# Small weights of an output pipeline moved to the right end of SBUF

## The chip, the cores and the metric

The kernel runs on one core of a Trainium2 chip. The metric is device time of one execution in microseconds (us); lower is better. A core has five engines with their own instruction streams: PE (TensorE, matmuls into PSUM), DVE (VectorE), ACT (ScalarE), POOL (GpSimd) and SP (SyncE, which here only issues DMA transfers). ACT issues a few transfers too. Each stream runs in program order; streams wait for each other and for transfers through semaphores.

## The reference

Eight images of 64x64 positions and 96 channels go through two layers. Each layer is a residual block: group norm, a projection to 192 + 192 channels (x and z), a 3x3 depthwise convolution with SiLU on x, a selective scan over the 4096 positions in four directions with 16 states a channel, layer norm, a gate by SiLU of z, and a projection back to 96 channels. Cut to what matters:

```python
xz = x @ in_proj_w.T;  xp, z = xz[..., :Di], xz[..., Di:]
xc = silu(depthwise_conv3x3(xp) + conv_b)
# selective scan, for each of 4 directions:
h = exp(delta * A) * h + delta * B * u
y = sum(h * C) + u * D
# output
y = layernorm(y, norm_g, norm_b)
x = x + (y * silu(z)) @ out_proj_w.T
```

The second layer has the same parts, and its scan comes from a cumulative-sum form whose result is far from zero only near the ends of each direction, so the kernel computes short heads of it.

## The kernel before

**Stages.** For every image `b` the kernel runs `scan_rows` (from L423): the first layer's scan of image `b`, with the short second-layer scan of image `b-1` and the next convolutions woven in. Then `between(b)` (from L1775) runs the output pipeline `out_phase` (from L1461) as a transition to the next scan. There are eight scans and seven transitions (`b` = 0 to 6); a last `finish` ends the program. In the transitions from `b` = 1 on, `out_phase` carries two streams of eight chunks of 512 positions each: the first layer's output of image `b` (chunks 0 to 7), and the second layer's output of image `b-1` (chunks 8 to 15). In the transition after image 0 it carries one. The order of all work is written out by hand: a counter `k` steps through the list `order`, in which each stage of a chunk has a lag (`row` 8, `silu` 7, `product` 9, `project` 10, `end` 10, `store` 11), so stages of several chunks alternate.

**The end of a transition.** The last chunk passes, among others: the second sum of squares on POOL (L1599), the row-picking matmul `ps_r` on PE with weights `w_pick` (L1534), which spreads one row of reciprocal deviations over 96 partitions, the gate SiLU on ACT (L1589, z weights `zw`, bias `zb`, result `sz`), the scaling on DVE (L1610), the affine step on ACT (L1577), the gated product on POOL (L1602, which reads `sz`), the output matmul on PE (L1562), the residual sum on DVE (L1647) and the store, issued from ACT for the second layer (L1648) and from SP for the first (L1703).

**The start of a scan.** SP issues, in this order: dt_rep and dtu_rep (L518), three pairs b_rep and c_rep (L528), the next dt_rep and dtu_rep, the fourth pair, then the low rows x_dbl (L549) and the `edged` rows of a convolution (L1012). The first twelve are 512 KB each. On ACT the scan starts with the copy `drive` (L878) and decays (L861); behind the first two decays stands the step L614 on the result of the matmul `ps_dt` (L602), which reads x_dbl. On DVE each set is one product (L895) and one scan (L908).

**Memory.** Tiles come from pools; pools are stacked from the left end of SBUF or, with `side="right"`, from the right end, and are released when their block ends. A later pool may lie on the bytes of an earlier one; then its first use waits for the last users of the earlier tiles there. `out_phase` puts its short-lived tiles in a pool called `before` (right end, through the argument `brief`) and its other tiles in `final` (left side). Addresses in one partition, in the transitions with two streams:

| tile or pool | bytes |
|---|---|
| `final`: w_pick, zw1, zb, r, sz (three buffers) | 158,368 to 177,120 |
| `before`: zw0, sums, squares, dt0, z0 and others | 182,496 to 229,344 |
| next scan: dt_rep, two buffers | 176,096 to 184,288 |
| next scan: dtu_rep, two buffers | 184,288 to 192,480 |
| next scan: b_rep and c_rep, nine buffers | 192,480 to 229,344 |

The end of sz's third buffer and the beginning of dt_rep's first share 1,024 bytes. In this program the first dt_rep load waits for the last product (L1602) and the last `ps_r` (L1534).

**Transfers.** All transfers of SP and ACT take their completion semaphore from one rotation of eight, in the order in which the program was laid out, and each first waits for the previous transfer on its semaphore.

Of the kernel before, what the change touches and what calls it, by code (L numbers as in the profile page):

```python
# [8 lines left out]
F32 = mybir.dt.float32  # L9
# [6 lines left out]
NB, HH, WW, C = 8, 64, 64, 96  # L16
L = HH * WW
NH = 2
# [35 lines left out]
def two_ss2d_layers(ctx: ExitStack, tc: tile.TileContext, t: dict, out: bass.AP):  # L54
# [92 lines left out]
    def load_late(pool, *names):  # L147
        for name in names:
            w[name] = pool.tile(list(t[name].shape), F32, name=f"w_{name}")
            nc.sync.dma_start(w[name], t[name])  # L150
# [11 lines left out]
    def chunk_stats(st, i, chunk):  # L162
        nc.vector.bn_stats(st[:, i, :], chunk)

    def stats_tile():
        return small.tile([C, L // MM, nc.vector.BN_STATS_DIM], F32, name="bn_st")

    def group_norm_stages(st, bank):

        got = {}  # L170

        def one(name, **more):
            got[name] = small.tile([C, 1], F32, name=f"gn_{name}", **more)
            return got[name]

        def across(name, src):
            got[name] = bank(f"ps_{name}")
            nc.tensor.matmul(got[name][:C, 0:1], w["group"], src, start=True, stop=True)

        def aggregate():  # L180
            got["mv"] = small.tile([C, nc.vector.BN_AGGR_DIM], F32, name="bn_mv")
            nc.vector.bn_aggr(got["mv"], st)

        def means():
            across("pm", got["mv"][:, 0:1])

        def tiny(out, src, func=AF.Identity, **more):
            nc.scalar.activation(out, src, func, **more)
            return out

        def deviations():
            mv, gm = got["mv"], one("less", bufs=2)
            tiny(gm, got["pm"][:C, 0:1], scale=-1.0 / 3.0)
            dev = tiny(one("dev"), mv[:, 0:1], AF.Square, bias=gm)
            tiny(dev, dev, bias=mv[:, 1:2])

        def variances():
            across("pv", got["dev"])

        def variance():  # L200
            tiny(one("gv"), got["pv"][:C, 0:1], scale=1.0 / 3.0, bias=eps_ln[:C])

        def root():

            r, p, gm = one("r", bufs=8), one("p"), one("gm", bufs=8)
            tiny(r, got["gv"], AF.Ln)
            tiny(r, r, AF.Exp, scale=-0.5)
            tiny(p, r, AF.Square)
            tiny(p, p, scale=got["gv"])
            tiny(p, p, scale=-0.5, bias=one_half)  # L210
            tiny(r, r, scale=p)
            tiny(one("shift", bufs=8), got["less"], scale=r)
            tiny(gm, got["less"], scale=-1.0)

        return [aggregate, means, deviations, variances, variance, root], got
# [1242 lines left out]
                    stop=i == NS - 1,  # L1458
                )

    def out_phase(*streams, plan=None, brief=None):  # L1461

# [6 lines left out]
        with (  # L1471
# [7 lines left out]
            chunks = L // MM  # L1479
            n = len(streams) * chunks  # L1480
            brief = brief or pool
            load_late(pool, "pick")
            zw, zb = [], []
            for l, *_ in streams:
                home = brief if l == 0 and len(streams) > 1 else pool
                zw.append(home.tile([C, D], F32, name=f"zw{l}"))
                nc.sync.dma_start(zw[-1], t[f"in{l}"][:, D:])
                zb.append(pool.tile([C, NH], F32, name=f"zb{l}"))
            plan = plan(pmm) if plan else {}
            held = [{} for _ in range(n)]  # L1490
            groups = [{} for _ in range(n // Q)]
# [181 lines left out]
    def first_deltas(b, xc, pool, bank):  # L1673

        units, jobs, sets, x_dbl = parts = scan_parts(b)
        stages = projection(xc, x_dbl, units[0], pool, bank)
        for job in jobs[:NH]:
            stages += ready(xc, x_dbl, job, pool, bank, by_pe=False)
        stages += projection(xc, x_dbl, units[1], pool, bank)
        return parts, [stage for _, stage in stages]  # L1680
# [16 lines left out]
    def finish_first(b, y, st, xpool):  # L1697


        def done(i, ps, x):  # L1700
            nc.vector.tensor_tensor(x, ps, x, ALU.add)
            chunk_stats(st, i, x)
            return lambda: nc.sync.dma_start(x1[b][:, i * MM : (i + 1) * MM], x)  # L1703

        return 0, norm0[b], y, loaded(t["x"][b], xpool), done
# [57 lines left out]
    def second_of(b, pool, brief, xpool, put):  # L1763

        return finish_second(norm1[b], short_sum(b, pool, brief, put), loaded(x1[b], xpool), out[b])

    def planner():
        plan = {}

        def put(step, stage, *args):  # L1770
            plan.setdefault(step, []).append(lambda: stage(*args))

        return plan, put

    def between(b, y):  # L1775

        st = stats_tile()
        xc = maps[b + 1]
        with (
            tc.tile_pool(name="before", bufs=1, side="right") as before,  # L1780
            tc.tile_pool(name="xs", bufs=1) as xpool,
            tc.tile_pool(name="behind", bufs=1) as pool,
        ):
            plan, put = planner()

            streams = [finish_first(b, y, st, xpool)]
            if b >= 1:
                streams.append(second_of(b - 1, pool, before, xpool, put))
            found = {}

            def beside(pmm):
                bank = lambda name: pmm.tile([P, MM], F32, tag="mm", name=name)
                found["parts"], stages = first_deltas(b + 1, xc, before, pmm)
                steps = (1, 2, 2, 3) + (4, 5, 5, 6, 6, 7, 7, 6, 8, 9, 9)
                steps += (8, 9, 9, 10, 10, 11, 12, 14, 15, 16, 16) + (11, 12, 12, 13)
                for step, stage in zip(steps, stages, strict=True):
                    put(step, stage)
                stages, found[1] = group_norm_stages(st, bank)
                put(24, nc.scalar.preload_act_table_set, "natural_log_exp_and_others")
                for step, stage in zip((17, 18, 19, 20, 21, 24), stages, strict=True):  # L1800
                    put(step, stage)
                if b + 2 < NB:
                    ahead = stats_tile()
                    pieces = []

                    def piece(i):
                        pieces.append(before.tile([C, MM], F32, name="x_st", bufs=3))
                        nc.sync.dma_start(pieces[i], t["x"][b + 2][:, i * MM : (i + 1) * MM])

                    for i in range(L // MM):  # L1810
                        put(i + 3, piece, i)
                        put(i + 5, lambda i: chunk_stats(ahead, i, pieces[i]), i)
                    stages, found[0] = group_norm_stages(ahead, bank)
                    for step, stage in zip((13, 14, 15, 16, 17, 18), stages, strict=True):
                        put(step, stage)
                return plan

            out_phase(*streams, plan=beside, brief=before)
            for kind, norm, image in ((1, norm1, b), (0, norm0, b + 2)):
                if kind in found:  # L1820
                    norm[image] = tuple(found[kind][x] for x in ("gm", "r", "shift"))
        return xc, found["parts"]

    def finish(b, y):

        st = stats_tile()
        with tc.tile_pool(name="behind", bufs=1) as pool:
            plan, put = planner()
            streams = [finish_first(b, y, st, pool)]
            if b >= 1:  # L1830
                streams.append(second_of(b - 1, pool, pool, pool, put))
            out_phase(*streams, plan=lambda pmm: plan)
        with tc.tile_pool(name="x1T", bufs=1) as pool1:
            x1T = pool1.tile([C, L], F32, name="x1T")
            nc.sync.dma_start(x1T, x1[b])
            xc = keep.tile([C, NH, L], F32, name="map")
            norm = conv_second(x1T, st, xc)
            with rotating():
                scan_head(xc, worst)
            out_phase(finish_second(norm, xc, kept(x1T), out[b]))  # L1840
# [37 lines left out]
    with tc.manual_schedule():  # L1878
        for b in range(NB):
            y = keep.tile([C, NH, L], F32, name="map")  # L1880
            with (
                tc.tile_pool(name="rows", bufs=1) as rows,
                tc.tile_pool(name="beside", bufs=1) as pool,
            ):
                scan_rows(xc, y, parts, beside(b, pool), rows, pool)
            if b + 1 < NB:
                xc, parts = between(b, y)
# [101 lines left out]
```

## Time and profile before

| what | value |
|---|---|
| runs | 12389.48, 12404.24, 12425.54 us; median 12404.24 |
| the profiled execution | 12404.1 us, its span 12402.2 us |
| busy PE, DVE, ACT, POOL | 77%, 88%, 78%, 85% of the span |
| DMA, share of 16 engines | 44.6% on SP's queue, 0.3% on ACT's |
| granted TensorE clock | 0.803 |
| one POOL product L1602 (96x1024) | 2.35 us |
| one DVE scan L908 (128x1024), with state | 2345 ns |

The span is the time from the first to the last instruction of one profiled execution. A line of the profile's lists names a source line, an engine, the operation with its output and input tiles, a count, the busy time and the mean of one, and then the idle time of that engine just before these instructions, with what ended it (the releaser). The engines are busy most of the time on average, and this average hides the transitions, in which they take turns; a change inside one is read in the order of time.

### The profile page before, as it was taken

What the parts mean: (1) busy time and instruction counts of PE and PEld (TensorE: products, weight loads), DVE (VectorE), ACT (ScalarE), POOL (GpSimd) and SP (SyncE); (2) the same over time, 40 slices, a digit from 0 to 9 for tenths busy, and PEclk for the clock granted to TensorE, in tenths of its full rate; (3) what the DMA queues carried; (4) which work ended last, traced back from release to release, by engine and by line L of the source; (5) the groups of instructions that cost most, each with busy time, mean ns of one, the idle gap of its engine ahead of it and who ended that gap; (6) DMA issues with size and microseconds to landing.
All of it is one profiled execution on the core that took longest, in us unless ns stands there. A gap on an engine that the chain in (4) does not pass through costs nothing. (4 is left out here: it accounts for less than half of the span.)

```text
span 12402.2 us, 134216 instructions
## 1 busy us (share of the span) xinstructions
PE 9540.3 (77%) x44312; PEld 3022.4 (24%) x44312; DVE 10960.4 (88%) x6870; ACT 9688.3 (78%) x15131; POOL 10508.3 (85%) x4802
## 2 busy tenths in 40 slices
PE   5875578787888778877788777888788887886565
PEld 1221122222222222222222222222222222222122
DVE  6999889996999969999799987999879998899976
ACT  4888778887887868878788787887778877788874
POOL 3999889996999969998699986999879987799974
PEclk8887778888888878888888878887788877887786
DMA  3444344444444444444444454444544445444430
GB/s 96 165 155 156 127 159 161 154 156 152 148 164 160 161 138 164 163 162 147 148 156 158 162 165 135 160 162 161 163 138 153 156 156 158 136 165 160 157 123 23
DMA packets 666561, 1853.80 MB, mean 149 GB/s; under 512 B 184936, under 2 KB 199150, under 8 KB 665757
## 3 DMA queue, kind: packets, MB, share of 16 engines
q1 hardware_dynamic: 658685, 1832.52, 44.6%
q10 hardware_dynamic: 7168, 12.59, 0.3%
q8 instruction: 352, 5.77, 0.2%
q14 instruction: 356, 2.92, 0.1%
HBM read 1533.82 MB, written 311.02 MB: 149 GB/s over the span
## 5 line engine op out<-in xcount | busy, mean ns | idle before, releaser
L924 POOL TENSOR_TENSOR out<-set,c_rep 128x1024 f32<-128x1024 f32 x3114 | 7290.0, 2359 | 884.4 <-PE acc L960 317.8
L908 DVE TENSOR_TENSOR_SCAN set<-decay,state,set 128x1024 f32<-128x1024 f32 x2304 | 5366.3, 2345 | 407.4 <-ACT decay L861 189.6
L861 ACT ACTIVATE decay<-dt_rep,w_a 128x1024 f32<-128x1024 f32 x3072 | 3420.2, 1114 | 335.7 <-DVE set L908 329.8
L895 DVE TENSOR_TENSOR set<-drive,b_rep 128x1024 f32<-128x1024 f32 x2346 | 2811.1, 1198 | 43.1 <-DMA b_rep<-x_dblr 28.2
L1027 PE MATMUL ps_conv<-edged,taps 96*96 96x512 f32 (+1 forms) x4032 | 2476.3, 754 | 54.5 <-DVE dt L787 25.9
L960 PE MATMUL acc<-out,w_gather 128*32 128x256 f32 x24576 | 2274.2, 480 | 8.1 <-POOL out L924 7.7
L908 DVE TENSOR_TENSOR_SCAN set<-decay,set 128x1024 f32<-128x1024 f32 x768 | 1744.4, 2286 | 224.5 <-ACT decay L861 146.6
L885 POOL TENSOR_TENSOR set<-dtu_rep,b_rep 128x1024 f32<-128x1024 f32 x768 | 1810.1, 2357 | 93.9 <-DMA b_rep<-x_dblr 51.6
L951 PE MATMUL acc<-map,w_eye 96*32 96x256 f32 x4608 | 568.5, 575 | 1483.4 <-ACT map L990 1253.5
L990 ACT COPY map<-acc 32x256 f32<-32x256 f32 x3072 | 1470.5, 479 | 45.8 <-PE acc L960 5.6
L960 PEld LDWEIGHTS acc<-out,w_gather 128*32 128x32 f32 x24576 | 781.8, 130 | 1939.5 <-issue 1282.0
L1027 PEld LDWEIGHTS ps_conv<-edged,taps 96*96 96x96 f32 (+1 forms) x4032 | 727.5, 200 | 1405.4 <-issue 1244.3
L919 ACT COPY state<-set 128x1 f32<-128x1 f32 x2304 | 426.1, 185 | 754.3 <-DVE set L908 747.9
L634 PE MATMUL ps_sp<-z,w_eye 96*96 96x512 f32 x960 | 658.2, 774 | 288.8 <-ACT ln L643 244.4
L655 POOL TENSOR_TENSOR dtu<-ln,map 96x1024 f32<-96x1024 f32 x256 | 670.7, 2620 | 237.2 <-DVE ln L651 133.0
L878 ACT COPY drive<-dtu_rep 128x1024 f32<-128x1024 f32 (+1 forms) x810 | 808.0, 997 | 34.7 <-DMA dtu_rep<-dtu_far 30.1
L602 PE MATMUL ps_dt<-x_dbl,w_dtw 7*96 7x512 f32 x1024 | 595.4, 663 | 301.2 <-ACT z L615 151.0
L951 PEld LDWEIGHTS acc<-map,w_eye 96*32 96x32 f32 x4608 | 101.4, 121 | 1954.6 <-ACT map L990 1656.1
L634 PE MATMUL ps_sp<-dtu,w_eye 96*96 96x512 f32 x960 | 554.6, 662 | 0.0
L634 PE MATMUL ps_sp<-ln,w_eye 96*96 96x512 f32 x960 | 535.5, 642 | 0.0
L614 ACT ACTIVATE dt<-ps_dt 96x512 f32<-96x512 f32 x512 | 303.0, 592 | 279.2 <-PE ps_dt L602 260.0
L634 PE MATMUL ps_sp<-dt,w_eye 96*96 96x512 f32 x960 | 506.7, 610 | 0.0
(239 smaller groups left out, 9496.8 us busy)
## 6 DMA issues: line engine op xcount, KB each, us to landing
dt_rep<-dt_far SPq DMA_DIRECT2D x768, 512.0 KB
dtu_rep<-dtu_far SPq DMA_DIRECT2D x768, 512.0 KB
b_rep<-x_dblr SPq DMA_DIRECT2D x256, 512.0 KB
c_rep<-x_dblr SPq DMA_DIRECT2D x256, 512.0 KB
b_rep<-x_dblc SPq DMA_DIRECT2D x256, 512.0 KB
c_rep<-x_dblc SPq DMA_DIRECT2D x256, 512.0 KB
dt_far<-ln SPq DMA_DIRECT2D x256, 384.0 KB
dtu_far<-dtu SPq DMA_DIRECT2D x256, 384.0 KB
```

The lines of the kernel that those rows point to most:

```text
L634: nc.tensor.matmul(job["ps"][:C, :], w["eye"], job[term][:, halves[s]], start=i == 0, stop=i == 3,)
L655: nc.gpsimd.tensor_tensor(like(job["dtu"], col), like(job["dt"], col), positions(xc[:, h, :], col, t0, T), ALU.mult,)
L861: nc.scalar.activation(s["decay"], s["group"]["dt"], AF.Exp, scale=rate)
L878: nc.scalar.copy(s["group"]["drive"], s["group"]["dtu"])
L885: nc.gpsimd.tensor_tensor(s["buf"], s["group"]["dtu"], b, ALU.mult)
L895: nc.vector.tensor_tensor(s["buf"], s["group"]["drive"], b, ALU.mult)
L908: nc.vector.tensor_tensor_scan(ordered(s["buf"], unit), ordered(s["decay"], unit), ordered(s["buf"], unit), 0.0 if unit["nth"] == 0 else s ...
L924: nc.gpsimd.tensor_tensor(s["out"], s["buf"], s["unit"]["c", s["i"]], ALU.mult)
L951: nc.tensor.matmul(acc, lhs[:, GC * g : GC * (g + 1)], positions(old[:, h, :], unit["column"], unit["t0"] + at, n), start=True, stop=False ...
L960: nc.tensor.matmul(acc, w["gather"], s["out"][:, at : at + n], start=False, stop=s["i"] == NS - 1, skip_group_check=True,)
L990: nc.scalar.copy(yk, like(acc, unit["column"]))
L1027: nc.tensor.matmul(job["ps"][:C, :], taps[l][:k, h, tap, :], edged[:k, tap // 3 : tap // 3 + rows, tap % 3 : tap % 3 + WW], start=tap == 0 ...
```

## The change

`out_phase` takes one more pool, `late`, and puts w_pick, the z weights zw (except the zw of the first stream, which stay in `brief` when there are two streams) and the biases zb there. `between` opens it on the right side before all other pools of the transition. Without the argument, in `finish` and elsewhere, `late` is `final`, as it was.

```diff
-    def out_phase(*streams, plan=None, brief=None):
+    def out_phase(*streams, plan=None, brief=None, late=None):
...
             brief = brief or pool
-            load_late(pool, "pick")
+            late = late or pool
+            load_late(late, "pick")
             zw, zb = [], []
             for l, *_ in streams:
-                home = brief if l == 0 and len(streams) > 1 else pool
+                home = brief if l == 0 and len(streams) > 1 else late
                 zw.append(home.tile([C, D], F32, name=f"zw{l}"))
                 nc.sync.dma_start(zw[-1], t[f"in{l}"][:, D:])
-                zb.append(pool.tile([C, NH], F32, name=f"zb{l}"))
+                zb.append(late.tile([C, NH], F32, name=f"zb{l}"))
...
         with (
+            tc.tile_pool(name="late", bufs=1, side="right") as late,
             tc.tile_pool(name="before", bufs=1, side="right") as before,
...
-            out_phase(*streams, plan=beside, brief=before)
+            out_phase(*streams, plan=beside, brief=before, late=late)
```

With two streams, `late` then takes 226,976 to 229,344, `before` 180,128 to 226,976, and `final` ends at 174,752. The loops, the operations and their order stay as they are.

## The prediction

> **What bounds the kernel now.** I read the list of what SyncE's queue waited for first, because the diff moves only tiles, and a tile that changes its place can change only waits. Columns: engine and line, what it waited for, us in total, times, longest.
>
> ```profile
> SPq L518 <- PE ps_r L1534: 126.0, 6, 21.6
> SPq L518 <- POOL y L1602: 31.2, 6, 5.2
> ```
>
> L518 is the load of dt_rep and dtu_rep. Six times, once for each of the transitions after images 1 to 6, the queue stands idle until the last row-picking matmul (L1534) and then 5.2 us more, until POOL's last gated product (L1602). The transition after image 0 is not among them.
>
> Then one transition in order of time (after image 1; start us, us, engine, line):
>
> ```profile
> 3072.77 1.02 PE L1534 MATMUL ps_r<-r,w_pick 128*96 128x512 f32 x2
> ...
> 3076.68 2.34 POOL L1602 TENSOR_TENSOR y<-y,sz 96x1024 f32<-96x1024 f32 x1 [0.90 <-ACT y L1577]
> ...
> 3079.05 0.57 SPq L518 DMA_DIRECT2D dt_rep<-dt_far  x1
> ...
> 3082.09 0.32 ACTq L1648 DMA_DIRECT2D out<-x_in  x1
> ...
> 3084.82 1.02 ACT L878 COPY drive<-dtu_rep 128x1024 f32<-128x1024 f32 x1 [4.60 <-DMA dtu_rep<-dtu_far]
> ...
> 3089.97 0.44 SPq L549 DMA_DIRECT2D x_dbl<-x_dblr  x1
> ...
> 3094.00 1.20 DVE L895 TENSOR_TENSOR set<-drive,b_rep 128x1024 f32<-128x1024 f32 x1
> ...
> 3100.83 1.99 PE L602 MATMUL ps_dt<-x_dbl,w_dtw 7*96 7x512 f32 x2 [19.50 <-DMA c_rep<-x_dblr]
> ...
> 3105.06 2.29 DVE L908 TENSOR_TENSOR_SCAN set<-decay,set 128x1024 f32<-128x1024 f32 x1 [9.86 <-ACT decay L861]
> ```
>
> The product ends at 3079.02 and dt_rep is issued 0.03 us later. Twelve loads of 512 KB follow, then the small x_dbl load (L549). DVE does what the first loads allow, then is idle 9.86 us, for this reason: its fourth scan needs a decay that stands on ACT behind L614, L614 needs PE's L602, and L602 needs x_dbl. The label on L602's wait names c_rep, the neighbouring load; its operand is x_dbl.
>
> Last, the same stretch by windows (busy us of PE, PEld, DVE, ACT, POOL; granted clock; share of the 16 DMA engines; GB/s):
>
> ```profile
> 3074.00:3079.00 5.00, 3.66 (x8) 0.92 (x7) 2.16 (x3) 3.56 (x7) 4.10 (x2) 1.00 0.27 79
> 3079.00:3084.00 5.00, 1.93 (x4) 0.57 (x4) 0.95 (x2) 1.12 (x5) 0.02 (x1) 1.00 0.71 247
> 3084.00:3089.00 5.00, 0.00 (x0) 0.00 (x0) 1.94 (x2) 3.10 (x3) 0.17 (x1) 0.72 1.05 374
> 3089.00:3094.00 5.00, 0.00 (x0) 0.00 (x0) 4.90 (x4) 0.00 (x0) 3.61 (x4) 0.50 1.00 294
> 3094.00:3099.00 5.00, 0.00 (x0) 0.00 (x0) 1.20 (x2) 0.00 (x0) 0.00 (x0) 0.50 1.00 400
> 3099.00:3104.00 5.00, 2.00 (x3) 0.41 (x3) 0.00 (x0) 1.15 (x4) 4.64 (x2) 0.50 0.38 73
> ```
>
> From 3084 to 3099 the DMA engines are full; before 3079 they are a quarter busy and after 3104 idle. So a scan's head is a block of DMA work, about 20 us, that begins when SyncE may issue dt_rep and ends when x_dbl has landed. No compute engine bounds it. Its start decides.
>
> **What the Trainium skill says.** "DMA: Bandwidth & Descriptors", section "Issuing engines are not separate DMA queues": transfers started by ScalarE and SyncE run on the same 16 engines and interleave. The trace agrees: output stores from ACT's queue move in the midst of the loads (0.39 MB, 3.8% of the 16 engines, in 3079 to 3106). The same page, "Queues, rings and completion order": a DMA engine takes turns between the queues that have work, packet by packet. The store issued at 3082.09 fits that: it does not wait for the loads ahead of it, which last to 3100; the load at 3088.71 that must wait for its landing gets through after 6.6 us (5.8 to 7.8 in the other five transitions). "SBUF — State Buffer", section "SBUF: two separate sides": transfers and engines use separate ports, so loads that start earlier should not slow the products and affine steps still running. No run yet shows that.
>
> **The change part by part.** The built programs before and after hold the same instructions in the same order on every engine. What differs is addresses and waits.
>
> 1. *The wait of the first dt_rep load, six transitions.* Before: last ps_r (PE) and last product (POOL L1602), because sz's third buffer ends at byte 177,120 and dt_rep's begins at 176,096. After: sz ends at 174,752, and the load waits for the last ps_r (its pick is now at the right end, inside the region of the loads), the last silu (L1589), and the last second sum on POOL. In the trace of before the silu ends at 3071.94, the second sum earlier, ps_r at 3073.80. So dt_rep can go at 3073.83 instead of 3079.05: 5.22 us. The other five transitions give 5.22 to 5.23. Six times 5.22 is 31.3 us, which is the 31.2 of the first fence.
>
> 2. *What the earlier block meets.* Two output stores lie in the block before; now the one issued at 3076.49 does too. Two stores take 3.8% of 27 us, 1.03 us, of all engines, so one takes 0.51 us. Net per transition 5.22 − 0.51 = 4.71 us.
>
> 3. *The order of landings.* Each transfer waits for the one eight earlier in a common rotation of semaphores. As dt_rep now precedes the last two output stores, the rotation shifts: the seventh load waits for dtu_rep instead of dt_rep, the eighth for the store issued at 3076.49, the twelfth for the one at 3079.89, x_dbl for the one at 3082.09, and that store, on ACT, for the first dt_rep. By before's durations: the store of 3082.09 finds dt_rep landed by about 3079 (the second load was usable 5.2 us after its issue); x_dbl can go at 3082.09 + 6.6 = 3088.7, some 7 us before the block ends near 3096.1, so it is still queued behind loads. Seven loads are out by 3079.6 and the eighth by about 3082, while the engines, at about 1.6 us a load, have done four by then: they do not run dry. Cost taken: 0; bounds 0 and 4.7, the whole gain, if the store lands too late.
>
> 4. *ACT, DVE and PE at the head.* ACT cannot copy drive before its last store at 3082.09 + 0.32 = 3082.41, so its first three sets gain only 2.4 us. That stays off the path: they end at 3095.20 − 2.4 = 3092.8, and the fourth scan comes at 3105.06 − 4.7 = 3100.4. New waits for the last product stand on ACT (L614) and DVE (L895); it ends at 3079.02, before either is reached.
>
> 5. *Start of the transition.* The loads of pick and the z weights lose the wait for the last gathering matmul, and the y1 load behind them takes it up. On SyncE's queue all stand behind the ys_far store (2941.24, then pick at 2941.80), which needs that matmul's result anyway; pick's first reader comes at 2971.7. Cost 0. If that cover went, it would be the three short issues, 1.3 us.
>
> 6. *First transition.* Its dt_rep now waits for ps_r, which ends at 1544.96; the queue reaches it only after the x1 store at 1560.29. Cost 0. The last image has no `late` pool: 0.
>
> 7. *Tiles 2,368 bytes further down*: nothing in this trace tells what an address costs an instruction. Taken as 0; bounds −5 and +5 us in all, about 0.5% of the 993 us that the seven transitions last.
>
> From x_dbl on, every engine's work follows in program order, so the shift stays. Sum: 6 × 4.71 = 28.3 us. The profiled execution took 12404.1 us (span 12402.2); its time equals the median of the runs, 12404.2. Forecast: 12404.1 − 28.3 = **12376 us**, 0.23% less. A measurement of this kernel can tell about 0.3%, 37 us, from no change, so the likeliest result lies just inside.
>
> **Rivals.**
>
> *Larger gain.* From dt_rep's issue to L602 the six transitions take 21.8, 23.7, 22.5, 22.5, 22.8 and 21.5 us, mean 22.5. If the reordered issue brings all to the shortest, 1.0 us more is won each time, and without the charge of step 2 that is 6.2 × 6 = 37 us: 12367. For: the slices of the block vary from 294 to 400 GB/s when full. Against: the same bytes move.
>
> *Gain eaten.* x_dbl lands no earlier than now because the loads or stores it waits for come later. At 0 to 3 us a transition: 12386 to 12404. The change not doing what it says belongs here; the waits of the built program speak against it.
>
> *Slower.* The same lane: x_dbl behind the last output store. This store cannot be issued before 3082.09. Once it lands later than about 3098.5, 16.4 us after issue instead of 6.6, x_dbl comes later than today's 3100.8; at 22.6 us each transition loses 6.2, in sum 37: 12441. For: more loads are outstanding when it is issued. Against: the turns between queues seen above.
>
> **How the numbers follow.** The likeliest case (gain 20 to 37 us) 0.51; larger gain 0.30, which includes what the scatter of runs (12389 to 12426) adds at this edge; gain eaten 0.13; slower 0.06. Faster by over 0.3% is the larger gain, 0.30; within 0.3% is 0.51 + 0.13 = 0.64; slower 0.06. The likeliest's own range is 12367 to 12384. The range for 8 in 10 leaves out the upper tail of the larger gain and the slower case: 12352 to 12408.
>
> **What would show it.** L518's wait for L1602 gone from SyncE's list, its wait for ps_r left at 126; dt_rep issued within 0.1 us of the last ps_r's end; L602 4 to 5 us earlier after the last product (21.8 us now), DVE's idle before the fourth scan shorter by about 2.3 us. Wrong if x_dbl is issued later than about 12 us after the last product, if the DMA share drops inside the block, or if product and affine take longer beside the loads.

## The result, and the profile after

| what | before | after |
|---|---|---|
| median of 20 runs each | 12408.47 us | 12380.05 us |
| lowest to highest | 12371.43 to 12436.94 | 12348.02 to 12414.69 |
| the profiled execution, its span | 12404.1, 12402.2 us | 12396.2, 12394.4 us |
| granted TensorE clock | 0.803 | 0.805 |

The ratio of after to before is 0.998, with a 95% interval of 0.997 to 0.9989: 25 us less, between 14 and 37; the medians differ by 28.4. The profiled execution of after took 16 us more than the median. The two spans therefore differ by only 8 us, and what follows compares the transitions and not the spans: within one execution, the time from one transition's third scan to the next's varies by up to 20 us.

In the source of after the lines from L1482 on have moved down by one, those from L1780 on by two (ps_r is L1535, the product L1603, the store L1649). First, what SyncE's queue waited for, in after (us in total, times, longest):

```profile
SPq L518 <- PE ps_r L1535: 124.9, 6, 21.4
...
SPq L528 <- DMA out<-x_in: 18.8, 9, 3.0
...
SPq L528 <- DMA dtu_rep<-dtu_far: 12.9, 6, 2.4
```

The line for the product, 31.2 us in six waits, is gone from the list. The wait for ps_r stays, 124.9 us where it was 126.0. New is how much the b and c loads (L528) wait for the landing of output stores: 18.8 us, against 7.9 before.

Then the transition after image 1 in order of time, in after (start us, us, engine, line):

```profile
3077.26 1.02 PE L1535 MATMUL ps_r<-r,w_pick 128*96 128x512 f32 x2
...
3078.41 0.57 SPq L518 DMA_DIRECT2D dt_rep<-dt_far  x1
...
3081.17 2.34 POOL L1603 TENSOR_TENSOR y<-y,sz 96x1024 f32<-96x1024 f32 x1 [0.90 <-ACT y L1578]
...
3086.58 0.32 ACTq L1649 DMA_DIRECT2D out<-x_in  x1
...
3087.00 1.02 ACT L878 COPY drive<-dtu_rep 128x1024 f32<-128x1024 f32 x1 [2.30 <-DVE x_in L1648]
...
3094.01 0.28 SPq L549 DMA_DIRECT2D x_dbl<-x_dblr  x1
...
3101.78 1.99 PE L602 MATMUL ps_dt<-x_dbl,w_dtw 7*96 7x512 f32 x2 [15.96 <-DMA c_rep<-x_dblr]
...
3106.07 2.29 DVE L908 TENSOR_TENSOR_SCAN set<-decay,set 128x1024 f32<-128x1024 f32 x1 [9.72 <-ACT decay L861]
```

The last ps_r ends at 3078.28 and dt_rep goes at 3078.41, 2.76 us before the last product even starts. The product ends at 3083.51, and L602 comes 18.27 us after it, where it came after 21.81. The chain from x_dbl over L602 to the scan is as it was.

The same stretch by windows in after (busy us of PE, PEld, DVE, ACT, POOL; granted clock; share of the 16 DMA engines; GB/s):

```profile
3078.00:3083.00 5.00, 4.12 (x9) 1.14 (x8) 2.05 (x3) 3.14 (x5) 4.10 (x2) 1.00 0.78 224
3083.00:3088.00 5.00, 1.95 (x5) 0.57 (x4) 1.37 (x2) 2.54 (x9) 0.51 (x1) 0.97 1.01 376
3088.00:3093.00 5.00, 0.00 (x0) 0.00 (x0) 4.69 (x4) 2.10 (x3) 0.00 (x0) 0.50 1.02 308
3093.00:3098.00 5.00, 0.00 (x0) 0.00 (x0) 3.34 (x2) 0.00 (x0) 3.67 (x4) 0.50 1.03 403
```

POOL's products and the full DMA engines now share the first window, in which POOL is as busy (4.10 us) as in the corresponding window before, with the DMA at 0.78 instead of 0.27. The block of DMA work has slid under the end of the pipeline.

All six transitions, in us from the end of the last product, and the length of the block from dt_rep's issue to L602; means of the six:

| kernel | dt_rep goes | block | L602 | third scan |
|---|---|---|---|---|
| before | +0.03 | 22.47 | 22.50 | 26.73 |
| after | −5.10 | 23.66 | 18.57 | 22.86 |

The start came 5.13 us earlier and the block grew by 1.19 us: L602 is 3.93 us earlier, six times that is 23.6 us. The third scan starts 3.87 us earlier, in sum 23.2 us. That is within the interval of the runs, 14 to 37 us.

A slip of the prediction has to be named before its words are used again: the scan at 3105.06 us that it calls the fourth is, counted in the trace, DVE's third of that scan stage (before at 9.3 and 12.8 us after the product come the first two). What it says of its decay holds for the third. Here it is called the third.

### The profile page after: what moved, and what is told of

It is laid out like the page before. It is cut to its first block, busy times and chain, and to the rows that moved or that the text cites. A ratio compares the mean times of both kernels' runs of the same rounds, so it can differ in the third digit from the quotient of the medians.

```text
span 12394.4 us, 134241 instructions
## 1 busy us (share of the span) xinstructions
PE 9546.8 (77%) x44312; PEld 3027.5 (24%) x44312; DVE 10958.3 (88%) x6870; ACT 9692.8 (78%) x15131; POOL 10509.2 (85%) x4802
## 5 line engine op out<-in xcount | busy, mean ns | idle before, releaser
L908 DVE TENSOR_TENSOR_SCAN set<-decay,state,set 128x1024 f32<-128x1024 f32 x2304 | 5365.6, 2345 | 407.4 <-ACT decay L861 191.0
L908 DVE TENSOR_TENSOR_SCAN set<-decay,set 128x1024 f32<-128x1024 f32 x768 | 1743.8, 2286 | 222.2 <-ACT decay L861 150.7
L878 ACT COPY drive<-dtu_rep 128x1024 f32<-128x1024 f32 (+1 forms) x810 | 808.0, 998 | 18.8 <-DVE x_in L1648 13.8
L602 PE MATMUL ps_dt<-x_dbl,w_dtw 7*96 7x512 f32 x1024 | 596.8, 664 | 279.9 <-ACT z L615 151.2
```

The lines of the kernel that those rows point to most:

```text
L878: nc.scalar.copy(s["group"]["drive"], s["group"]["dtu"])
L908: nc.vector.tensor_tensor_scan(ordered(s["buf"], unit), ordered(s["decay"], unit), ordered(s["buf"], unit), 0.0 if unit["nth"] == 0 else s ...
```

## The experiments

The theory is that only one thing counts: whether the left pool reaches into dt_rep's bytes, since the first load then waits for the last user of that whole pool, the product. The first rival is that the changed addresses of the other tiles, the moved pools at the right end or the new order of completion semaphores bring the gain. Three kernels change the place of the tiles only.

**Row-picking weights alone at the right end** (against after; the left pool ends at 175,584):

```diff
-                home = brief if l == 0 and len(streams) > 1 else late
+                home = brief if l == 0 and len(streams) > 1 else pool
...
-                zb.append(late.tile([C, NH], F32, name=f"zb{l}"))
+                zb.append(pool.tile([C, NH], F32, name=f"zb{l}"))
```

> The changed kernel with only the row-picking weights in the pool at the right end; the z weights and their biases are in the left pool again. The left pool then ends at byte 175,584, 512 bytes below the first dt_rep buffer. Theory (what counts is only whether the left pool reaches into the buffer of the first load): the wait for the last product stays away, dt_rep goes at the end of the last ps_r, each of six transitions is 3.9 us shorter from the last product to L602, in sum 20 to 28 us less than the kernel before, as in the changed kernel. Rival (the changed addresses of the other tiles, or the place of the z weights, bring the gain): the tiles move by about two thirds as far as in the change, so about 16 us, or nothing if the z weights bring it.

Measured: ratio 0.9979 (0.997 to 0.9989), median 12373.63 against 12399.47 us. dt_rep goes 5.15 us before the product, the block takes 24.36 us, the third scan comes at 23.50.

**z weights alone at the right end** (against after; the left pool ends at 176,288, 192 bytes too high):

```diff
-            load_late(late, "pick")
+            load_late(pool, "pick")
```

> The mirror of it: the changed kernel with only the z weights and biases at the right end; the row-picking weights are in the left pool again. The left pool ends at byte 176,288, 192 bytes above the beginning of dt_rep's first buffer. Theory: the wait for the last product (about 5.2 us, six times) is back in SyncE's list, and the time is that of the kernel before, 12408 us within 10 us. Rival (addresses or the place of the z weights): a third of the gain or more, 10 to 28 us less than before.

Measured: ratio 0.9996 (0.9987 to 1.0006). What SyncE's queue waited for in this kernel:

```profile
SPq L518 <- PE ps_r L1535: 123.9, 6, 21.2
...
SPq L518 <- POOL y L1603: 31.2, 6, 5.2
```

The wait is back in full, six times 5.2 us, for an overlap of 192 bytes. The left pool of the kernel above ends 704 bytes lower, and there the wait is gone; the overlap's size does not matter (192 bytes here, 1,024 in before).

**A pad under the left pool** (against after; the weights stay at the right end, the left pool ends at 177,120 again):

```diff
             brief = brief or pool
             late = late or pool
+            if late is not pool:
+                pool.tile([C, 592], F32, name="pad")
```

> The changed kernel with an unused tile of 2,368 bytes a partition at the bottom of the left pool, in the seven transitions. The weights are at the right end and the pool there has moved as in the change, but the left pool's other tiles are back at their old addresses, and it ends at 177,120 again. Theory: the wait for the last product is back (31 us in sum), time as before, 12408 within 10 us. Rival (the pools at the right end, or the order of completion semaphores, bring the gain): 20 to 28 us less than before, as in the changed kernel.

Measured: ratio 0.9993 (0.9982 to 1.0004). The same list for this kernel:

```profile
SPq L518 <- PE ps_r L1537: 124.2, 6, 22.3
...
SPq L518 <- POOL y L1605: 31.2, 6, 5.2
```

Again dt_rep goes 0.03 us after the product, the block takes 22.63 us, and the third scan comes at 26.89 us. The moved pools at the right end by themselves bring nothing that can be measured. With these three the cause of the gain is settled by the traces: it is the wait. What the addresses are worth besides cannot be told from zero, but the intervals of the two kernels that wait reach to 16 and 22 us less than before. The order of the completion semaphores is not tested apart from the wait: where the wait is back, so is the old order, in which dt_rep follows the store that is issued 2.5 us before it. The 5.13 us of the earlier start are read from SyncE's list itself and do not hang on that order.

**Why the block grew.** In after, four output stores move in the block instead of two. Two kernels take the bytes out of the stores and leave their number and order, one made from after, one from before:

```diff
-            return lambda: nc.scalar.dma_start(dst[:, i * MM : (i + 1) * MM], x)
+            n = 8 if i >= 4 else MM
+            return lambda: nc.scalar.dma_start(dst[:, i * MM : i * MM + n], x[:, :n])
```

> The changed kernel in which the output stores of the last four chunks of each transition write 8 of 512 columns (the rest of these chunks is not stored). The number and order of transfers stay. Theory (a block of loads lasts as long as the bytes that move in it, and in the changed kernel four output stores of 0.2 MB lie in it): the block from dt_rep's issue to L602 shrinks from 23.7 us by four stores of 0.55 us, 2.2 us, to about 21.4; six times 2.2 is 13 us less than the changed kernel, 37 to 41 us less than the kernel before. Rival (the block is long because x_dbl waits for the landing of the last store): the store lands at once, x_dbl is issued 3 us or more earlier, but the loads queued ahead still decide; or, if the landing did decide, more than 3 us per transition, over 18 us in sum.

> The kernel before in which the output stores of the last four chunks of each transition write 8 of 512 columns (the rest of these chunks is not stored). Here two of the four stores lie in the block of loads, and the seventh and eighth loads wait for earlier loads, not for stores. Theory (the bytes of a store lengthen the block by its share of the DMA engines, about 0.5 us): the block from dt_rep's issue to L602 shrinks by 1.0 us, from 22.5 to about 21.5 us in the mean; 6 us in sum, 12402. Rival (in the changed kernel it is the waits of the seventh and eighth loads for output stores that lengthen its block, and the bytes count for little): the block stays within 0.4 us of 22.5, and the time at 12408.

Measured: from after, ratio to before 0.9986 (0.9978 to 0.9994); from before, 0.9996 (0.9983 to 1.0008). The theory (bytes at their share) failed in size: in the first kernel the block is 0.94 us shorter than in after, where it asked for 2.2, and in the second it is 0.48 us longer than in before, where it asked for 1.0 us shorter. The block of one transition by DMA queues, the window set from dt_rep's issue to L602 (packets, MB, share of 16 engines; q1 is SP's queue, q10 ACT's). In after:

```profile
q1 hardware_dynamic: 2620, 6.54, 85.5%
q10 hardware_dynamic: 448, 0.79, 9.5%
```

In the kernel with thin stores made from after:

```profile
q1 hardware_dynamic: 2622, 6.54, 85.3%
q10 hardware_dynamic: 448, 0.01, 1.1%
```

The loads' share did not rise into the room that the stores left: 85.5% and 85.3%. Here are the means over six transitions, with the time that the packets of the stores filled and the time that no packet filled, both as shares of the 16 engines. (Full windows read up to 1.05, so packet times overlap a little, and the empty time is rather more than stated.)

| kernel | block | stores fill | empty |
|---|---|---|---|
| before | 22.47 us | 1.03 | 2.01 |
| z weights alone (waits for the product) | 23.02 us | 1.03 | 2.53 |
| pad (waits for the product) | 22.63 us | 1.03 | 1.91 |
| thin stores, from before | 22.95 us | 0.13 | 3.20 |
| after | 23.66 us | 2.22 | 1.73 |
| row-picking weights alone (does not wait) | 24.36 us | 2.22 | 2.76 |
| thin stores, from after | 22.72 us | 0.25 | 2.95 |

A store's bytes thus have no fixed price. Taken out of before, they left the block no shorter than in the three kernels that wait for the product; the engines were only empty for longer. Taken out of after, 1.97 us of bytes made the block 0.94 us shorter, or 1.64 us against the row-picking kernel, whose stores are the same. The means of blocks scatter from kernel to kernel, and the six blocks of this thin kernel alone range from 20.7 to 24.1 us, so half a microsecond is not resolved. The runs do not show the shorter block at all: by the ratios this kernel is 17 us faster than the kernel before and after is 25 us faster, and the intervals overlap. But the growth by one to two microseconds is there in both kernels that do not wait.

Not all four stores move beside the loads. The first of them is issued 0.23 us before dt_rep. This is the whole list of DMA queues in after for the first 1.35 us from dt_rep's issue (3078.41 to 3079.76 us):

```profile
q10 hardware_dynamic: 103, 0.19, 48.7%
```

So 103 of this store's 112 packets start before any packet of a load. In all six transitions the first load packet starts 1.34 to 1.37 us after dt_rep's issue, when about nine tenths of that store are through. It fills time in which the engines stand empty in before, and beside the loads move three stores, one more than in before.

What makes up the rest of the growth is open. The rival of the second expectation (waits for landings) is not excluded. In after the seventh and eighth loads go 6.17 and 9.38 us after dt_rep, in before 4.11 and 5.85; and from the fourth to the sixth microsecond the engines of after are 0.96, 0.89 and 0.90 full, those of before 1.04, 1.03 and 0.98. The thin stores do not part the two: they landed hardly sooner, so the eighth load, which waits for one of them, still goes at 8.82 us, and x_dbl goes at 15.0 us in both kernels. As the block is short there all the same, these waits alone do not lengthen it. In both thin kernels, with the late eighth load and without, a gap shows in the fifth microsecond after dt_rep's issue, where the engines are 0.75 to 0.76 full in the mean of six; it was not followed further.

**Seven buffers of x_in.** If the theory is right, any way to shorten the left pool takes the wait away, and one that puts nothing that ps_r reads at the right end takes that wait away too. This kernel is made from before:

```diff
-            x = xpool.tile([C, MM], F32, name="x_in", bufs=8)
+            x = xpool.tile([C, MM], F32, name="x_in", bufs=7)
```

Its control adds an unused tile, so that the left pool ends at 177,120 as before:

```diff
+            if brief is not pool:
+                pool.tile([C, 512], F32, name="pad")
             load_late(pool, "pick")
```

> The kernel before (its weights all in the left pool) with seven buffers of x_in instead of eight: the left pools then end at byte 175,072, below dt_rep, and nothing stands in the pool at the right end that the last ps_r reads. Theory (a first load waits for the last user of every pool that its buffer overlaps, and for nothing else): dt_rep waits neither for ps_r nor for the product but for the last root step on DVE and the last variance matmul, and goes some 19 us before the last product (before: 0.03 us after it, changed kernel: 5.1 us before it). The block of loads then runs beside the pipeline's last stages and ends about with it; x_dbl waits for the landing of the last store (issued 3.1 us after the product, landed 2 to 4 us later with an empty queue), so L602 starts 7 to 10 us after the product instead of 22.5: six times 12 to 15 us, 72 to 90 us less than before, near 12325. Rival 1 (transfers slow the pipeline beside them, or a buffer less of x_in makes chunks wait): half of it or nothing comes back in longer last stages; 12360 to 12430. Rival 2 (only the place of the weights matters): as before.

> The control to it: seven buffers of x_in as well, and an unused tile of 2,048 bytes a partition at the bottom of the left pool, which ends at 177,120 again. Theory: seven buffers cost nothing by themselves (chunks are loaded 5 steps after the first stage and stored at step 11, so at most seven are alive), the wait for the last product is back, and the time is that of the kernel before, 12408 within 10 us. Rival (seven buffers change the transitions by themselves, for better or worse): more than 10 us away from it.

Measured: ratio 0.9943 (0.992 to 0.9965) with seven buffers, median 12342.99 against 12410.68 us; 0.9998 (0.9986 to 1.001) for the control. The kernel with seven buffers beats both. One of its transitions in order of time:

```profile
3058.83 0.57 SPq L518 DMA_DIRECT2D dt_rep<-dt_far  x1
...
3075.49 2.34 POOL L1602 TENSOR_TENSOR y<-y,sz 96x1024 f32<-96x1024 f32 x1 [0.90 <-ACT y L1577]
...
3080.91 0.32 ACTq L1648 DMA_DIRECT2D out<-x_in  x1
...
3086.34 0.28 SPq L549 DMA_DIRECT2D x_dbl<-x_dblr  x1
...
3088.38 1.99 PE L602 MATMUL ps_dt<-x_dbl,w_dtw 7*96 7x512 f32 x2 [8.23 <-DMA x_dbl<-x_dblr]
...
3092.67 2.29 DVE L908 TENSOR_TENSOR_SCAN set<-decay,set 128x1024 f32<-128x1024 f32 x1 [2.06 <-ACT decay L861]
```

dt_rep goes 19.0 us before the product ends (3077.83). The loads run beside the last stages, and the block is over when the pipeline is. What remains is x_dbl: it is issued 5.4 us after the last store (3.7 to 5.4 in the six, where the expectation had 2 to 4), and SyncE's list names what it waits for in this kernel:

```profile
SPq L549 <- DMA out<-x_in: 39.5, 9, 7.1
```

x_dbl lies on x_in's bytes, so it waits until the last output store has landed. In the mean of six transitions L602 comes 9.88 us after the product and the third scan 14.17, 12.56 earlier than before; six times that is 75 us, against 68 in the medians.

The loads slow the stages beside them little. The windows of this kernel, in which all of this overlaps:

```profile
3063.00:3068.00 5.00, 5.00 (x13) 1.95 (x13) 2.42 (x3) 4.42 (x8) 3.77 (x2) 1.00 1.00 365
3068.00:3073.00 5.00, 4.99 (x12) 1.71 (x11) 2.44 (x4) 2.79 (x5) 3.12 (x2) 1.00 1.03 281
3073.00:3078.00 5.00, 3.48 (x8) 0.90 (x6) 2.16 (x3) 3.72 (x8) 3.93 (x2) 1.00 1.01 391
```

The last column but one is the DMA share, full in all three, and the last products take 2.34 to 2.37 us each, as they do alone. From the first product to the last one of a transition it takes 99.6 us in the mean, against 97.8 in before and 98.2 in the control. Single transitions range from 94 to 103 us in all three, so the difference of 2 us is not told from nothing, and it is small against 12.6 of gain. This agrees with the separate ports of the Trainium skill's "SBUF — State Buffer", section "SBUF: two separate sides", of which the prediction had to say that no run showed it yet.

**x_dbl away from x_in.** Made from the kernel with seven buffers:

```diff
             tc.tile_pool(name="loads", bufs=2, side="right") as loads,
+            tc.tile_pool(name="low", bufs=1, side="right") as rows,
             tc.tile_pool(name="piece", bufs=1) as piece,
```

> The kernel with seven x_in buffers, and x_dbl in a pool of its own directly below the loads at the right end (bytes 172,000 to 176,096) instead of at the left, where it lies on x_in. In the kernel with seven buffers x_dbl is issued 6.7 to 8.5 us after the last product, because it waits for the landing of the last output store; L602 follows at 8.7 to 10.6 us and DVE's third scan at 13.0 to 14.8 us. Theory (there the last store's landing sets the third scan): x_dbl now waits for the product and the load before it only, goes about 2 us after the product, L602 starts by 4 to 5 us, and the third scan comes as soon as DVE has done the first two sets, at 12.9 us; six times 1.3 us is 8 us less than with seven buffers alone, some 75 us less than the kernel before. Rival (POOL is the next bound: its memsets of the edged rows wait for the same landing, and its first output and early set stand behind them): the third scan comes earlier, the fourth does not, and the time stays as with seven buffers alone, 67 us less than before.

Measured: ratio 0.9944 (0.9926 to 0.9962), median 12329.21 against 12402.58 us. In order of time (one line further down in the source than with seven buffers; the product ends at 3049.75):

```profile
3051.13 0.43 SPq L550 DMA_DIRECT2D x_dbl<-x_dblr  x1
...
3057.48 1.99 PE L603 MATMUL ps_dt<-x_dbl,w_dtw 7*96 7x512 f32 x2 [5.43 <-DMA x_dbl<-x_dblr]
...
3062.62 4.68 DVE L909 TENSOR_TENSOR_SCAN set<-decay,set 128x1024 f32<-128x1024 f32 x2
```

x_dbl goes 1.4 us after the product, 0.03 to 3.9 in the six, and the third scan comes at 12.88 us in the mean: DVE is never idle from the first set to it, so nothing is left to win before the third scan by loads. The fourth scan, which the rival had stand still behind POOL, moved too, from 17.42 to 15.41. By the trace this is 8 to 12 us in all; by the runs it is not told apart from seven buffers alone (73 and 68 us less than before, with intervals of 20 us or more to either side). One number of the expectation was off: L602 started 5.6 to 8.6 us after the product and not 4 to 5, since x_dbl, though issued early, took some 5 us to land.

## Why the prediction was right

The forecast was 12376 us and 28.3 us less; the medians differ by 28.4, and the time is 12380, since before's median over 20 runs is 12408. The mechanism is shown. That the medians agree to 0.1 us is luck: the ratio of the runs stands for 25 us and the six transitions of the trace for 23, because two terms of the sum were off, by 0.8 us in a transition together, and the runs do not resolve that.

1. *The wait of the first dt_rep load*: right in place, number and size. L518's wait for the product is gone, 31.2 us in six; the three placements show that the gain comes and goes with this wait. dt_rep goes 0.13 us after ps_r and not 0.03 (the sign asked for was within 0.1), so the start moved by 5.13 us and not 5.22.
2. *What the earlier block meets*: this step was mis-sized. It charged 0.51 us for one more store, and the block grew by 1.19. The count came out right: two more stores fall into the block, but one of them is nine tenths through before a load's first packet starts. The price did not. The premise that each store costs its share of the engines fell with the thin stores, and the store is not all that changed, since the seventh and eighth loads go later too. Where the other 0.7 us come from is open. The net gain is 3.93 us in a transition and not 4.71, so the sign "L602 4 to 5 us earlier" was just missed.
3. *The order of landings*: right in the main, with less room than thought. The seventh and eighth loads go 6.2 and 9.4 us after dt_rep in the mean, where the working gave 5.8 and 8.2; x_dbl goes 15.0 us after dt_rep, where it gave 14.9. The DMA share in the full five-microsecond windows is 1.01 to 1.03, but in the mean of six it falls to 0.89 in the fifth microsecond of the block, where before has 1.03; over three microseconds this comes to about 0.3 us, so the cost taken as 0 was small and not nothing. The rival *slower* had this lane too; x_dbl came 8.9 to 11.1 us after the product, short of the 12 at which the prediction was to be wrong. One reading on the way was too strong: the store of 3082.09 was said not to wait for the loads ahead of it, "which last to 3100". Only five loads were issued before it, and by the packets four and a half of them were through when the store was, at 3088.23. In the six transitions it overtook between a quarter of a load and one load. It takes turns, but the loads that last to 3100 stand behind it.
4. *ACT, DVE and PE at the head*: wrong in its result for DVE, off the path. drive comes 2.3 us earlier after the product, as said (3.49 instead of 5.80). But the first scan gains 3.5 us and not 2.4, since before the first product on DVE also waited for b_rep (its wait names b_rep in four of the six transitions), which now has landed by then. With a third scan that gains 3.9, DVE's idle before it is 9.72 us, hardly shorter than 9.86 (0.4 us shorter in the mean of six); the prediction's sign of 2.3 us less did not come.
5. *Start of the transition* and 6. *first transition*: cost nothing, as said. From the end of the last long scan (L908) to the last product the six transitions take 180.5 us in the mean after and 180.6 before; in the first one L602 comes 30.84 us after the product, 30.42 before.
7. *Tiles further down*: nothing that can be measured for the tiles at the right end, which stay moved in the kernel with the pad; for those of the left pool it is not tested apart from the wait.

Of the rivals, *larger gain* and *slower* did not come. *Gain eaten* came in small: a quarter of the 5.13 us was given back in the block, while x_dbl was issued when the working had it.

## What to carry to other kernels

When a first load waits for a stage's last instruction, look up which bytes the two share before moving work: here 192 bytes were worth the same 5.2 us as 1,024, and each of the three ways to make room (after, the row-picking weights alone, a buffer of x_in less) took the wait away. Then ask what the load waits for next; the change traded one gate for another 5 us earlier (ps_r, because the moved weights lie under the loads), while a buffer less elsewhere set the gate 19 us earlier and was worth more than twice as much. Follow the lane to the next waiter, too, as x_dbl behind the last store here.

## What the runs showed that was not expected

- The wait goes by whole pools and not by the bytes that overlap. In after, dt_rep (from byte 176,096) goes 0.13 us after the last ps_r, though the weights that ps_r reads lie at 226,976, under the last b and c buffers and 42 KB above dt_rep's two. And before, the load waited for the product of chunk 15, though of sz's three buffers, taken in turn, the one that overlaps holds chunk 14, whose product ended 3.2 us earlier.
- Output stores of 0.2 MB have no fixed price beside a block of loads. Taking the bytes of two (1.03 us of all engines) out of before shortened nothing; taking four out of after (2.22 us, of which about 0.5 had moved before the first load packet) shortened the block by about one microsecond, which the runs do not resolve.
- Loads start slowly. In before and after dt_rep's first packet starts 1.34 to 1.37 us after its issue, and in after a store issued just ahead of it moves almost wholly in that time.
- The 28 KB of x_dbl took 2.0 to 2.3 us from issue to L602 with seven buffers of x_in, where the loads were over, and 4.7 to 6.3 us in the last kernel, where they were still moving. Issued 5.8 us earlier in the mean, it was in use only 2.5 us earlier.
